# A four-block network on one Trainium2 core: the third block finishes its pairs of heads one pipeline step on, merges start two turns later, and ScalarE copies projections and u out of PSUM

## The chip, the cores and the metric

The kernel runs as one program on one core of a Trainium2 chip. The metric is the time of the program on the device in microseconds (us). The core's engines are named as in its profile: PE is TensorE, DVE VectorE, ACT ScalarE, POOL GpSimd, SP SyncE, which here only issues DMA transfers.

## The reference

A network of four residual blocks on x of 4 x 512 x 512, each `x = x + layernorm(block(layernorm(x)))`: a state-space block, a block with top-2 experts, a delta-rule attention and a block whose experts are chosen per sequence. The change is in the third alone. Of that block (16 heads of 128 channels, 512 tokens, everything in float32):

```python
q = silu(conv4(x @ Wq)); k = silu(conv4(x @ Wk)) * D ** -0.5; v = silu(conv4(x @ Wv))
alpha = sigmoid(x @ Wa + ba); beta = sigmoid(x @ Wb + bb)
def step(St, inp):                      # over the tokens
    sk = einsum('bhij,bhj->bhi', St, k_)
    err = sk - v_
    Sn = a_ * St - b_ * err[..., None] * k_[..., None, :]
    o_ = einsum('bhij,bhj->bhi', Sn, q_)
    return Sn, o_
o = layernorm_per_head(o) * ln_w + ln_b
g = sigmoid(x @ Wg)
return (o * g) @ Wo
```

`conv4` is a causal convolution over 4 tokens, one channel at a time.

## The kernel before

The four blocks run one after the other; the third, `delta_rule`, takes about 1143 to 3400 us of the profiled execution. It works on one sequence at a time (4 of them, 512 tokens, `xT` channel-major) and on two heads at a time: 32 steps of one pair each, and one more to drain. The token recurrence is cut into 4 chunks of 128 tokens (`TPB`), each solved as a triangular system. In step n:

- First part, run in turns. `in_turns` takes one piece (up to a `yield`) of each generator after another. `prepare` for both heads of pair n: three projections (`project`, L151) with their convolution and silu (`conv_silu`: ACT L156, DVE three times L158, ACT L162, POOL L163), the products k k and k q within a chunk (L672), weighted with decays to `lt` and `pt` (L675), the diagonal blocks of `lt` written to DRAM (L679), scaled copies `kq` (L685) and `kt` (L692, L694). With them `merge` for pair n-1: it puts the 32 x 32 inverses in `yi` together to 128 x 128 ones in five pieces (L752 to L804), with PE and ACT or DVE in turn.
- Second part, in turns: `solve` for pair n, which inverts the 32 x 32 blocks row by row on DVE (62 instructions, L720 and L727) and sends them through DRAM into `yi` (L732, L736); and `recur` for pair n-1, four chunks of r (ACT copy L830), u (DVE copy L840), new state S (DVE L847, L850) and output o (ACT copy L858), each after small products (L817).
- Then `finish` for pair n-1: `stats` (DVE L114, L115, POOL L117, L118) and `normalise` (DVE L122) over the eight 128 x 128 tiles of `o`; for both heads the gate projection with `wg` (L151), its sigmoid (L892), the transposes of `o` (L895), scale and shift (ACT L897), the product with the gate (POOL L898); then the products with `wo` (L903), added into `y` (L907 for the first pair, L909 for the others). After the last pair of a sequence, `residual` adds the normalised `y` to x.

The order that the code is written in is not the order of the engines. Instructions are placed ahead of time by a list planner: the place in the program is the priority, and an instruction that the planner takes for ready earlier, on durations that it assumes, can pass those before it. So the gate projections (L151 with `wg`) stand between the small products of the recurrence in the trace. On the chip each engine then keeps that order, and waits on semaphores.

What can pass is limited by buffers. PSUM has three for projections, L672 and the products with `wo` (`mm`), three for transposes and merges (`tr`), two for the recurrence (`sq`). In SBUF `cv`, `sg`, `wh`, `wg` and `wo` have two each, `o` and `gt` one. All loads of this block are issued by SP, in one queue: `wh` (L941), `wg` (L874), `wo` (L876), the decays `ag` (L639), and the way through DRAM (L679, L710, L732, L736).

Of the kernel before, what the change touches and what calls it, by code (L numbers as in the profile page):

```python
# [16 lines left out]
P = 128  # L17
# [59 lines left out]
def network(ctx: ExitStack, tc: tile.TileContext, a: dict, out: bass.AP):  # L77
# [75 lines left out]
    def conv_silu(pool, dst, p, w, bias):  # L153

        cv = pool.tile([P, S], F32, tag="cv", name="cv", bufs=2)
        nc.scalar.activation(cv, p, AF.Identity, bias=bias, scale=w[:, 3:4])  # L156
        for j in range(1, 4):
            nc.vector.scalar_tensor_tensor(  # L158
                cv[:, j:], p[:, : S - j], w[:, 3 - j : 4 - j], cv[:, j:], ALU.mult, ALU.add
            )  # L160
        sg = pool.tile([P, S], F32, tag="sg", name="sg", bufs=2)
        nc.scalar.activation(sg, cv, AF.Sigmoid)  # L162
        nc.gpsimd.tensor_tensor(dst, cv, sg, ALU.mult)  # L163
# [417 lines left out]
    def delta_rule():  # L581
        with (
# [22 lines left out]
            def decays(xT):  # L605
# [3 lines left out]
                al = bp.tile([H2, TPB, CP], F32, tag="al", name="al")  # L609
                nc.gpsimd.memset(al[:, :, 0:1], 0.0)  # L610
                nc.scalar.activation(al[:, :, 1:], chunk(zp), AF.Sigmoid, bias=ba)
                ga = bp.tile([H2, TPB * CP], F32, tag="ga", name="ga")
# [24 lines left out]
            def prepare(h, w, xT, dd, nb, blocks, out):  # L637
# [5 lines left out]
                for j, dst in ((1, qk[:, 0, :]), (0, qk[:, 1, :]), (2, vT)):  # L643
                    p = ps("mm")
                    project(p, lambda k: w[:, k, j, :], xT)
                    conv_silu(sp, dst, p, cw[:, j, h, :], cb[:, j, h : h + 1])
                    yield
# [90 lines left out]
            def merge(lts, yi):  # L738
# [10 lines left out]
                lo, hi = slice(0, 2 * BK), slice(2 * BK, P)  # L749
                xx = sp.tile([P, UNITS, 2 * BK], F32, tag="xx", name="xx", bufs=1)  # L750
# [56 lines left out]
            def recur(heads, yi, o):  # L807

                st = None
                for cc in range(TPB):  # L810
# [29 lines left out]
                    nc.vector.tensor_copy(  # L840
# [40 lines left out]
            def finish(o, ws, wos, pair, xT, y):  # L881
# [5 lines left out]
                gated = []  # L887
                for j in range(2):
                    p = ps("mm")
                    project(p, lambda k: ws[j][:, k, :], xT)  # L890
                    gt = sp.tile([P, S], F32, tag="gt", name="gt", bufs=1)
                    nc.scalar.activation(gt, p, AF.Sigmoid)  # L892
                    p = ps("tr")
                    for cc in range(TPB):
                        nc.tensor.transpose(one(p, cc), o[:, cc, j, :], ident)  # L895
                    oT = sp.tile([P, S], F32, tag="oT", name="oT", bufs=2)
                    nc.scalar.activation(oT, p, AF.Identity, bias=lnb, scale=lnw)  # L897
                    nc.gpsimd.tensor_tensor(oT, oT, gt, ALU.mult)  # L898
                    gated.append(oT)
                for i in range(TPB):  # L900
# [7 lines left out]
                    else:  # L908
                        nc.vector.tensor_tensor(y[i], y[i], p, ALU.add)  # L909

# [14 lines left out]
            before = None  # L925
            for n in range(B * NPAIR + 1):
                b, pair = divmod(n, NPAIR)
                now, parts, heads = None, [], []
                if n < B * NPAIR:
                    if pair == 0:  # L930
# [3 lines left out]
                        y = [  # L934
                            bp.tile([P, D], F32, tag=f"y3{i}", name=f"y3{i}") for i in range(TPB)
                        ]
# [9 lines left out]
                    now = (heads, inverses[n % 2], b, pair, xT, y)  # L946
                if before:
                    gates = gate_weights(before[3])
                    parts.append(merge([head[0] for head in before[0]], before[1]))
                in_turns(*parts)  # L950
                parts = []
                if now:
                    parts.append(solve(blocks, now[1]))
                if before:
                    o = sp.tile([P, TPB, 2, P], F32, tag="o", name="o", bufs=1)
                    parts.append(recur([head[1] for head in before[0]], before[1], o))
                in_turns(*parts)
                if before:
                    finish(o, *gates, *before[3:])
                    if before[3] == NPAIR - 1:  # L960
                        for i in range(TPB):
                            residual(bp, before[2] * TPB + i, before[5][i])
# [230 lines left out]
```

## Time and profile before

| | |
|---|---|
| median of 3 runs | 3653.46 us (3652.5 to 3656.45) |
| profiled execution, its own time | 3652.81 us |
| its span in the trace | 3651.0 us |
| mean granted TensorE clock | 0.907 |
| busy PE / DVE / ACT / POOL | 3179.4 / 2064.8 / 799.0 / 953.5 us |
| third block | about 1143 to 3400 us |
| L151 with `wh` | 1536 products of 128 x 512, 607 ns each |
| L158 | 672, 744 ns each (576 of them in this block) |
| L903 | 512 products of 128 x 512, 738 ns each |
| L895 | 256 transposes, 467 ns each |

A float32 product appears as two records, so a projection of four products is eight. A row of the waits names the engine and line that waited, then who ended the wait, total us, times and longest. A row of the timeline gives start, duration, engine, line, operation, output and inputs, shape, how many were merged, and in square brackets the idle time before the first and who ended it. A product's own duration reaches past the start of the next one; how fast a row of them runs is read from start to start.

### The profile page before, as it was taken

To read this page: it belongs to the slowest core of one execution; us is meant where nothing else is said; L and a number is where in the kernel's file an instruction comes from. 1 tells how busy PE (TensorE), PEld (TensorE's weight loads), DVE (VectorE), ACT (ScalarE), POOL (GpSimd) and SP (SyncE) were. 2 spreads that over 40 slices of the span, in tenths; PEclk is the share of its full clock that TensorE was granted. 3 is DMA by queue.
4 is the path that set the end of the run, shared out by engine and by line. 5 is a ranking of instruction groups with operands and counts; after the bars stand their busy time and mean duration, and the time that the engine had idled before them with its cause. 6 is when DMAs were issued, how large, how long until landed. Compare 5 with 4: busy or idle time off the path is not lost.

```text
span 3651.0 us, 39495 instructions
## 1 busy us (share of the span) xinstructions
PE 3179.4 (87%) x13779; PEld 1752.8 (48%) x13779; DVE 2064.8 (57%) x5189; ACT 799.0 (22%) x1399; POOL 953.5 (26%) x1018
## 2 busy tenths in 40 slices
PE   7889989899995889989989989889899989897268
PEld 3333344455552455555555645555555545555123
DVE  4556441311125667676766666766676767664852
ACT  2223211111110222222222222222222222221111
POOL 1322120300016323322423222323223323221112
PEclk9889989999997889989989989989999989998679
DMA  6000010389973322322322322323322323220300
GB/s 239 0 1 0 0 50 0 137 285 319 319 262 93 81 63 60 90 60 54 82 63 64 89 59 53 83 60 80 73 60 64 78 60 77 69 60 22 107 12 35
DMA packets 281240, 316.23 MB, mean 87 GB/s; under 512 B 119073, under 2 KB 184993, under 8 KB 281042
## 3 DMA queue, kind: packets, MB, share of 16 engines
q1 hardware_dynamic: 266496, 277.62, 26.7%
q10 hardware_dynamic: 9426, 19.31, 1.4%
q0 software_dynamic: 5120, 16.78, 1.4%
q8 instruction: 110, 1.80, 0.2%
q14 instruction: 88, 0.72, 0.1%
HBM read 271.95 MB, written 41.68 MB: 86 GB/s over the span
## 4 chain that ended last, share of the span: by engine, by line
PE 75%; DVE 12%; POOL 6%; issue 3%; ACT 3%; DMA 2%; SPq 0%; POOLq 0%; ACTq 0%; DVEq 0%
PE mm L151 32%; PE sq L817 7%; PE mm L903 7%; PE mm L512 5%; PE mm L672 3%; PE sq L534 3%; PE sq L276 2%; POOL rs L118 2%; PE tr L358 2%; PE sq L1086 2%; DVE o L122 2%; DVE prod L997 2%; DVE term L720 1%; DVE st L114 1%; DVE xb L727 1%
## 5 line engine op out<-in xcount | busy, mean ns | idle before, releaser
L151 PE MATMUL mm<-xT,wh 128*128 128x512 f32 x1536 | 691.2, 607 | 2.2 <-DVE cv L158 2.0
L158 DVE SCALAR_TENSOR_TENSOR cv<-mm,prm,cv 128x511 f32<-128x511 f32 (+2 forms) x672 | 499.3, 744 | 289.2 <-ACT cv L156 275.1
L151 PEld LDWEIGHTS mm<-xT,wh 128*128 128x128 f32 x1536 | 294.4, 194 | 364.8 <-issue 357.6
L903 PE MATMUL mm<-wo,oT 128*128 128x512 f32 x512 | 293.9, 738 | 60.0 <-POOL oT L898 60.0
L156 ACT ACTIVATE cv<-mm,prm 128x512 f32<-128x512 f32 x224 | 172.6, 771 | 524.1 <-PE mm L151 516.7
L720 DVE TENSOR_TENSOR term<-lb,xb 128x60 f32<-128x60 f32 (+24 forms) x992 | 257.7, 260 | 20.5
L151 PE MATMUL mm<-xT,wg 128*128 128x512 f32 x512 | 262.2, 600 | 0.7 <-ACT gt L892 0.7
L727 DVE TENSOR_TENSOR xb<-xb,term 128x60 f32<-128x60 f32 (+24 forms) x992 | 223.7, 226 | 24.7
L903 PEld LDWEIGHTS mm<-wo,oT 128*128 128x128 f32 x512 | 120.0, 242 | 216.8 <-issue 139.2
L163 POOL TENSOR_TENSOR qk<-cv,sg 128x512 f32<-128x512 f32 x128 | 162.5, 1269 | 201.5 <-ACT sg L162 201.4
L895 PE MATMUL tr<-const,o 128*128 128x128 f32 x256 | 101.8, 467 | 111.9 <-DVE o L122 111.1
L162 ACT ACTIVATE sg<-cv 128x512 f32<-128x512 f32 x224 | 140.4, 627 | 256.6 <-DVE cv L158 255.6
L512 PE MATMUL mm<-gu,rT 128*128 128x352 f32 x624 | 190.9, 459 | 0.2 <-ACT rT L508 0.2
L151 PE MATMUL mm<-xT,gu 128*128 128x512 f32 (+1 forms) x384 | 176.2, 618 | 12.6 <-DVE act L353 12.6
L512 PEld LDWEIGHTS mm<-gu,rT 128*128 128x128 f32 x624 | 118.2, 190 | 76.5 <-issue 17.8
L817 PE MATMUL sq<-S,kq 128*128 128x128 f32 x768 | 154.5, 283 | 0.0
L117 POOL TENSOR_SCALAR rs<-mv 128x1 f32<-128x1 f32 (+2 forms) x112 | 30.9, 276 | 449.1 <-DVE mv L115 448.9
L672 PE MATMUL mm<-qk 128*128 128x128 f32 x1024 | 137.8, 283 | 6.3 <-POOL vT L163 2.9
L276 PE MATMUL sq<-w_out,G 128*128 128x512 f32 x256 | 128.0, 651 | 13.4 <-POOL G L272 11.7
L546 POOL DMA_INDIRECT got<-yg,index x32 | 38.1, 1189 | 362.5 <-DMA yg<-yo 345.4
L163 POOL TENSOR_TENSOR vT<-cv,sg 128x512 f32<-128x512 f32 x64 | 100.2, 1565 | 115.3 <-ACT sg L162 115.3
L672 PEld LDWEIGHTS mm<-qk 128*128 128x128 f32 x1024 | 123.9, 194 | 11.0 <-POOL vT L163 3.1
(231 smaller groups left out, 4891.2 us busy)
## 6 DMA issues: line engine op xcount, KB each, us to landing
gu<-in_gu SPq DMA_DIRECT2D x86, 704.0 KB
wh<-in_wh SPq DMA_DIRECT2D x64, 768.0 KB
ag<-dd SPq DMA_DIRECT2D x64, 516.0 KB
dn<-in_dn SPq DMA_DIRECT2D x43, 512.0 KB
wg<-in_wg SPq DMA_DIRECT2D x64, 256.0 KB
wo<-in_wo SPq DMA_DIRECT2D x64, 256.0 KB
lb<-blocks SPq DMA_DIRECT2D x128, 128.0 KB
xg<-zero SPq DMA_DIRECT2D x3, 3328.0 KB
```

Of the source, the lines that this page charges most:

```text
L151: nc.tensor.matmul(dst, lhsT=w(k), rhs=xT[:, k, :], start=k == 0, stop=k == n - 1)
L156: nc.scalar.activation(cv, p, AF.Identity, bias=bias, scale=w[:, 3:4])
L158: nc.vector.scalar_tensor_tensor(cv[:, j:], p[:, : S - j], w[:, 3 - j : 4 - j], cv[:, j:], ALU.mult, ALU.add)
L162: nc.scalar.activation(sg, cv, AF.Sigmoid)
L163: nc.gpsimd.tensor_tensor(dst, cv, sg, ALU.mult)
L276: nc.tensor.matmul(po, lhsT=G[ct][:, i * P : (i + 1) * P], rhs=w_out[:, ct, :], start=ct == 0, stop=ct == NCT - 1,)
L512: nc.tensor.matmul(dst, lhsT=rT[:, k, :], rhs=gu[:, k, lo : lo + F], start=k == 0, stop=k == KD - 1)
L672: nc.tensor.matmul(one(p, cc), lhsT=one(kT, cc), rhs=one(rhs, cc), start=True, stop=True)
L720: nc.vector.tensor_tensor(term, lb[:, i : i + 1, i + 1 :].to_broadcast([P, n, left]), xb[:, :n, i : i + 1].to_broadcast([P, n, left]), ALU ...
L727: nc.vector.tensor_tensor(rest, rest, term, ALU.add)
L817: nc.tensor.matmul(p[:, j, :], lhsT=lhsT, rhs=rhs, start=n == 0, stop=n == len(terms) - 1,)
L903: nc.tensor.matmul(p, lhsT=one(gated[j], i), rhs=wos[j], start=j == 0, stop=j == 1)
```

## The change

`finish` loses its first part, the statistics and normalisation of `o`, to a new function `centred`, which stays after the recurrence. What is left of `finish` becomes a generator and runs one step later, as the first of the parts that take turns with `prepare` and `merge`: pair n-2's gates and output products beside the projections of pair n. The loop gets one more step to drain. The loads of `wg` and `wo` move with it. `y` is allocated where it is first needed, and the residual of a sequence follows each product of the last pair. `o` and `gt` get two buffers; `al` and `ga` share the two of `xn`. `merge` waits two turns before its first piece. In this block `conv_silu` lets ScalarE copy the projection from PSUM into `sg`, and the convolution reads `sg`. The copy of u moves from VectorE to ScalarE.

```diff
--- before.py
+++ after.py
@@ -150,15 +150,19 @@
         for k in range(n):
             nc.tensor.matmul(dst, lhsT=w(k), rhs=xT[:, k, :], start=k == 0, stop=k == n - 1)
 
-    def conv_silu(pool, dst, p, w, bias):
+    def conv_silu(pool, dst, p, w, bias, apart=False):
+
 
         cv = pool.tile([P, S], F32, tag="cv", name="cv", bufs=2)
+        sg = pool.tile([P, S], F32, tag="sg", name="sg", bufs=2)
+        if apart:
+            nc.scalar.copy(sg, p)
+            p = sg
         nc.scalar.activation(cv, p, AF.Identity, bias=bias, scale=w[:, 3:4])
         for j in range(1, 4):
             nc.vector.scalar_tensor_tensor(
                 cv[:, j:], p[:, : S - j], w[:, 3 - j : 4 - j], cv[:, j:], ALU.mult, ALU.add
             )
-        sg = pool.tile([P, S], F32, tag="sg", name="sg", bufs=2)
         nc.scalar.activation(sg, cv, AF.Sigmoid)
         nc.gpsimd.tensor_tensor(dst, cv, sg, ALU.mult)
 
@@ -606,10 +610,10 @@
 
                 zp = ps("sq")[:H2, :]
                 project(zp, lambda k: wab[:, k, 0:H2], xT)
-                al = bp.tile([H2, TPB, CP], F32, tag="al", name="al")
+                al = bp.tile([H2, TPB, CP], F32, tag="xn", name="al", bufs=2)
                 nc.gpsimd.memset(al[:, :, 0:1], 0.0)
                 nc.scalar.activation(al[:, :, 1:], chunk(zp), AF.Sigmoid, bias=ba)
-                ga = bp.tile([H2, TPB * CP], F32, tag="ga", name="ga")
+                ga = bp.tile([H2, TPB * CP], F32, tag="xn", name="ga", bufs=2)
                 flat = al.rearrange("h c t -> h (c t)")
                 nc.vector.tensor_tensor_scan(ga, flat, c("pad1")[:H2], 0.0, ALU.mult, ALU.add)
                 dd = dram.tile([2, H2, TPB * CP], F32, tag="dd", name="dd")
@@ -643,7 +647,7 @@
                 for j, dst in ((1, qk[:, 0, :]), (0, qk[:, 1, :]), (2, vT)):
                     p = ps("mm")
                     project(p, lambda k: w[:, k, j, :], xT)
-                    conv_silu(sp, dst, p, cw[:, j, h, :], cb[:, j, h : h + 1])
+                    conv_silu(sp, dst, p, cw[:, j, h, :], cb[:, j, h : h + 1], apart=True)
                     yield
                 kT, qT = qk[:, 0, :], qk[:, 1, :]
 
@@ -747,6 +751,8 @@
 
                 q = [slice(n * BK, (n + 1) * BK) for n in range(NB)]
                 lo, hi = slice(0, 2 * BK), slice(2 * BK, P)
+                for _ in range(2):
+                    yield
                 xx = sp.tile([P, UNITS, 2 * BK], F32, tag="xx", name="xx", bufs=1)
                 nc.gpsimd.memset(xx[q[0], :, BK:], 0.0)
                 nc.vector.transpose(xx[q[0], :, :BK], yi[q[0], :, q[0]])
@@ -837,7 +843,7 @@
                         ),
                     )
                     u = sp.tile([P, 2, P], F32, tag="u", name="u")
-                    nc.vector.tensor_copy(
+                    nc.scalar.copy(
                         u, pair(lambda j, vT, pt, kq, gc, kt: [(yi[:, j * TPB + cc, :], r[:, j, :])])
                     )
                     if cc < TPB - 1:
@@ -878,25 +884,33 @@
                     wos.append(wo)
                 return ws, wos
 
-            def finish(o, ws, wos, pair, xT, y):
+            def centred(o):
 
                 rows = [(cc, j) for cc in range(TPB) for j in range(2)]
                 mv, rs = stats([o[:, cc, j, :] for cc, j in rows], EPS / P, "o")
                 for n, (cc, j) in enumerate(rows):
                     normalise(o[:, cc, j, :], o[:, cc, j, :], mv, rs, n)
-                gated = []
+
+            def finish(o, ws, wos, b, pair, xT, y):
+
+                gates = []
                 for j in range(2):
                     p = ps("mm")
                     project(p, lambda k: ws[j][:, k, :], xT)
-                    gt = sp.tile([P, S], F32, tag="gt", name="gt", bufs=1)
+                    gt = sp.tile([P, S], F32, tag="gt", name="gt", bufs=2)
                     nc.scalar.activation(gt, p, AF.Sigmoid)
+                    gates.append(gt)
+                    yield
+                gated = []
+                for j in range(2):
                     p = ps("tr")
                     for cc in range(TPB):
                         nc.tensor.transpose(one(p, cc), o[:, cc, j, :], ident)
                     oT = sp.tile([P, S], F32, tag="oT", name="oT", bufs=2)
                     nc.scalar.activation(oT, p, AF.Identity, bias=lnb, scale=lnw)
-                    nc.gpsimd.tensor_tensor(oT, oT, gt, ALU.mult)
+                    nc.gpsimd.tensor_tensor(oT, oT, gates[j], ALU.mult)
                     gated.append(oT)
+                yield
                 for i in range(TPB):
                     p = ps("mm")
                     for j in range(2):
@@ -907,6 +921,10 @@
                         nc.scalar.copy(y[i], p)
                     else:
                         nc.vector.tensor_tensor(y[i], y[i], p, ALU.add)
+                    if pair == NPAIR - 1:
+                        residual(bp, b * TPB + i, y[i])
+                    if i % 2:
+                        yield
 
             def in_turns(*parts):
                 parts = list(parts)
@@ -922,8 +940,9 @@
 
 
 
-            before = None
-            for n in range(B * NPAIR + 1):
+
+            before = last = None
+            for n in range(B * NPAIR + 2):
                 b, pair = divmod(n, NPAIR)
                 now, parts, heads = None, [], []
                 if n < B * NPAIR:
@@ -931,9 +950,6 @@
                         xT = bp.tile([P, KD, S], F32, tag="xT3", name="xT3", bufs=2)
                         norm_transposed(bp, xT, b)
                         dd, nb = decays(xT)
-                        y = [
-                            bp.tile([P, D], F32, tag=f"y3{i}", name=f"y3{i}") for i in range(TPB)
-                        ]
                     blocks = dram.tile([2, TPB, NB, BK, BK], F32, tag="blocks", name="blocks")
                     for j in range(2):
                         h = 2 * pair + j
@@ -943,23 +959,27 @@
                             a["wh"][h].rearrange("(k p) c -> p k c", p=P),
                         )
                         parts.append(prepare(h, w, xT, dd, nb, blocks[j], heads))
-                    now = (heads, inverses[n % 2], b, pair, xT, y)
+                    now = (heads, inverses[n % 2], b, pair, xT)
                 if before:
-                    gates = gate_weights(before[3])
                     parts.append(merge([head[0] for head in before[0]], before[1]))
+                if last:
+                    if last[2] == 0:
+                        y = [
+                            bp.tile([P, D], F32, tag=f"y3{i}", name=f"y3{i}") for i in range(TPB)
+                        ]
+                    o, at, of, x_of = last
+                    parts.insert(0, finish(o, *gate_weights(of), at, of, x_of, y))
                 in_turns(*parts)
-                parts = []
+                parts, last = [], None
                 if now:
                     parts.append(solve(blocks, now[1]))
                 if before:
-                    o = sp.tile([P, TPB, 2, P], F32, tag="o", name="o", bufs=1)
+                    o = sp.tile([P, TPB, 2, P], F32, tag="o", name="o")
                     parts.append(recur([head[1] for head in before[0]], before[1], o))
                 in_turns(*parts)
                 if before:
-                    finish(o, *gates, *before[3:])
-                    if before[3] == NPAIR - 1:
-                        for i in range(TPB):
-                            residual(bp, before[2] * TPB + i, before[5][i])
+                    centred(o)
+                    last = (o, *before[2:])
                 before = now
 
 
```

## Prediction

> **What bounds the kernel now.** I read the busy table first, then the waits of stage 3 (1143 to 3400 us), then one step of its loop in the timeline, then that step's granted clock. A 65 us step, one pair of heads, runs 32 times.
>
> The busy table, engine by engine:
>
> ```profile
> PE 3179.4 (87%) x13779; PEld 1752.8 (48%) x13779; DVE 2064.8 (57%) x5189; ACT 799.0 (22%) x1399; POOL 953.5 (26%) x1018
> ```
>
> TensorE is the busiest. The waits in stage 3 (total us, times, longest) name two places where TensorE itself stops:
>
> ```profile
> PE tr L895 <- DVE o L122: 111.1, 32, 3.9
> PE mm L903 <- POOL oT L898: 60.0, 32, 2.0
> ```
>
> That is 3.5 and 1.9 us, once per pair, both in `finish`. The larger waits in that list belong to ScalarE, GpSimd or the load queue, which have time to spare. The TensorE timeline of one step:
>
> ```profile
> 1837.60 0.61 PE L817 MATMUL sq<-const,vT 128*128 128x128 f32 x4
> 1841.65 3.24 PE L895 MATMUL tr<-const,o 128*128 128x128 f32 x8 [3.44 <-DVE o L122]
> 1846.75 10.13 PE L903 MATMUL mm<-wo,oT 128*128 128x512 f32 x16 [1.87 <-POOL oT L898]
> 1856.72 13.90 PE L151 MATMUL mm<-xT,wh 128*128 128x512 f32 x32
> ```
>
> The recurrence ends, TensorE waits 3.44 us, transposes at VectorE's pace, waits 1.87 us, and multiplies by `wo`. Then 16 products take 10.13 us where 32 of the same shape take 13.90 next (0.434 each, so 6.95 for 16). The cause is in the clock (columns: stretch, its us, PE busy, PEclk, DMA share, GB/s):
>
> ```profile
> 1370.00:1376.00 6.00, 5.05 (x7) 0.59 0.00 0
> 1376.00:1380.10 4.10, 4.10 (x11) 1.00 0.01 2
> ```
>
> After the pauses the clock is 0.59, then 1.00 again. Whole steps (PE, PEld, DVE, ACT, POOL busy, clock):
>
> ```profile
> 1906.70:1971.90 65.20, 59.44 (x322) 35.47 (x322) 45.05 (x131) 15.87 (x29) 19.75 (x21) 0.92 0.30 71
> 1971.90:2037.00 65.10, 59.29 (x322) 35.34 (x322) 44.81 (x130) 15.86 (x29) 19.82 (x21) 0.92 0.30 72
> ```
>
> What TensorE needs at full clock: `wh` 48 x 0.434 = 20.9; `wg` and `wo` 16 each, 6.95 twice; recurrence 84 x 0.111 = 9.3; L672 3.8; merge 4.2; transposes 1.7. Sum 53.8 of 65.2: 11.4 us per pair are lost.
>
> [...]0.59 after the pauses, 0.50 in 1777.2 to 1779.5. [...]in the step shown L720, two SBUF inputs, took 1.22 us where its neighbours took 0.23, until GpSimd's L898 (1845.44, 1.26 us) ended, within 0.1 us; L158, with its second input in PSUM, took 0.75 at 1864.90 beside GpSimd's L163. [...]The trace has 0.68 (L302, SBUF) against 0.745 (L158).
>
> **The change part by part.**
>
> 1. `finish` moves a step on. The transposes of `o` now follow both gate projections and four `wh` projections: 6 x 8 x 0.434 = 20.8 us of TensorE work that doesn't need `o`. Some is drawn into the recurrence, as all 16 `wg` products (6.9 us) are today, but at least 10 us must be left. From the recurrence's end (1838.2) to the last normalised `o` (1844.4) are 6.2 us: covered. Removed per pair: the wait 3.5; transposes at 3.24 instead of 8 x 0.11, 2.3; the wait for L898, 1.9, covered by the v projections (7 us) that follow in the same turn; the slow clock, from five steps (9.04, 9.10, 9.09, 10.13, 9.48; mean 9.37 - 6.95, less 0.1 by which the rows overlap), 2.3. **Sum 10.0.** If the v projections come earlier, the L898 wait stays.
> 2. `wg` and `wo` loads: still four per pair on SP, now in the step that uses them, behind the `wh` loads. SP stood 634.6 us in 58 waits for a `wo` buffer, longest 29.5; `ag`, `blocks<-lt`, `solved` and `yi` queue behind. At best this gains (in this step `solved` left at 1856.44, 1.7 after its data), at worst gates or blocks come late: -1 to +4 per pair, I take 0.
> 3. GpSimd: the same two L898 (2 x 1.28), now ahead of products for q, k, v; cover is 65 - 20 us of idle GpSimd. The same pow of L118; its 1.66 us is no longer waited for.
> 4. Merges two turns on: no instruction more. Their last two rounds lose the projections beside them: 2 x (ScalarE 0.58 + about 0.3 hand-over) = 1.8 us if nothing fills in; the first recurrence and gate products can. 0 to 3, I take 0.7. The reason to wait is in the profile: `yi` comes some 42 us after `lt` (1821.2 to 1863.4).
> 5. ScalarE copies: 192 x 0.586 (as L131, L907) and 128 x 0.372 for u: 3.5 + 1.5 per pair, plus 0.2 for an SBUF source; busy 16 to 21, of 56. Hidden by its idle time; a projection lags 0.6 us more, covered by three PSUM buffers. In exchange a PSUM buffer is free after one copy instead of after L156 and three L158. The u copies leave VectorE: -1.7; on the chain 0.37 for 0.42.
> 6. L158 from SBUF: 18 x 0.065 = -1.2 of VectorE; but L158 now contends with GpSimd. GpSimd's large instructions per pair: 6 x 1.27 + 4 x 0.95 + 2 x 1.05 + 2 x 1.28 = 16.1. Blocked time is from 0 to 16; VectorE spends some 28 of 56 us on two SBUF inputs (L158 12, solve 13, scans 2.5), half of the time, so 8, of which about 3 are paid today (L720's two of a microsecond, L658, L163). +5: VectorE 44.9 - 2.9 + 5 = 47 of 56. Not the bound, but late now and then: 0 to 5 on TensorE, I take 1.3.
> 7. `al` and `ga` share two `xn` buffers: four times, 0 to 3 us each. Second buffers for `o` and `gt`: nothing. The extra loop turn: its `finish` stood after the last recurrence before too. The last pair's gap stays: 31 gains.
>
> Net per pair 10.0 - 0.7 - 1.3 = 8.0, a step of about 57 us. 31 x 8.0 = 248. The profiled execution took 3652.81 (span 3651.0 and 1.8 around it); the median shown is 3653.46, within 0.65. 3652.8 - 248 = **3405 us**.
>
> **The rivals.** (A) The forecast, some 3320 to 3460. For it: outside the finish TensorE lost only about 1.4 us per step, so the order was good where it had work to draw on.
>
> (B) The gap is partly replaced. Either the merge's tail stands bare (3 us) with `yi` late[...]. Net 4 to 5.5 per pair: 3482 to 3529. For: the order is made ahead, from planned costs, and 20 us of VectorE idle stand in today's step. Against: ScalarE now empties PSUM, so TensorE can run up to five projections ahead of VectorE.
>
> (C) Slower[...]. Place: L158 with two SBUF inputs beside L163 and L685. Price: all 16.1 us blocked less the 3 paid, 44.9 - 2.9 + 13 = 55, and half of today's 20.3 us of idle remaining, 65.2; it decides when new waits and idle together pass 65.2 - 42 = 23.2 us per pair. With 13 of each it is 68: 31 x 2.8 = 87, 3740. For: L720 shows a wait to five times its length. Against: it needs nearly every GpSimd instruction to hit.
>
> (D) It doesn't do what it says: the planned order places gates and projections inside the recurrence and leaves the wait for `o`, moved but as long. Then only parts 5 and 6 act, within 10 us of 3653. Against: PSUM buffers bound what can be drawn ahead.
>
> **How the numbers follow.** A 0.68, B 0.22, C 0.06, D 0.04. D is split between 0.2% (7 us, about what a measurement of this kernel can tell from no change) and gains or losses beyond, C is slower: faster 0.91, same 0.03, slower 0.06. The low end is all of 10.0 and 0.8 of the 1.4 lost elsewhere, nothing paid: 31 x 10.8 = 335, 3318, rounded to 3320; the high end takes in B: net 4, 3530. Outside are C, D and the tails of A and B.
>
> **What would show it.** Right: the two finish waits gone (L895 on `o`, L903 on L898, together below 30 us), L895 near 280 ns a product, L903 near 600 instead of 738, clock above 0.96 in stage 3, a step of 56 to 58 us, ScalarE busy near 959. Part 6 shows as a longer L158 or L163. The forecast is wrong if TensorE waits over 4 us per step on L158, L163, `yi` or a `wg` load, or L158 averages over 1.1 us.

## The result, and the profile after

The changed kernel took **3705.0 us** (median of 4 runs, 3704.2 to 3714.9), the kernel before 3653.0 in the same comparison (4 runs, 3651.9 to 3656.5): ratio 1.0147, 95% interval 1.0129 to 1.0165. The forecast was 3405. The change made the kernel slower, by 52 us or 1.5%.

The busy table of the changed kernel, and then the shares of the chain that ended last, by engine:

```profile
PE 3171.8 (86%) x13779; PEld 1769.5 (48%) x13779; DVE 2129.5 (58%) x5061; ACT 952.2 (26%) x1719; POOL 988.1 (27%) x1018
```

```profile
DVE 29%; PE 26%; ACT 3%; POOL 3%; issue 3%; DMA 1%; SPq 0%; DVEq 0%; ACTq 0%; POOLq 0%
```

The busy shares hardly moved. The chain did: before, 75% of it were TensorE and 12% VectorE. Now VectorE has the larger part (these shares add up to 65%; the page gives no engine for the rest).

The waits of TensorE in the third block (1143 to 3460 us; total us, times, longest):

```profile
PE mm L917 <- POOL oT L911: 74.5, 38, 4.7
PE mm L676 <- DVE y L923: 50.1, 32, 2.3
PE tr L130 <- DVE xn L122: 49.9, 4, 16.0
PE tr L908 <- DVE o L122: 22.3, 19, 8.8
PE mm L917 <- ACT sg L159: 20.1, 9, 2.6
```

Line numbers have moved: L908, L911 and L917 were L895, L898 and L903; L676 was L672, L923 was L909, and L724, L731 were L720, L727. The convolution's multiply-adds are now L163 (L158 before), the silu's last product L167 (L163 before). L159 is the new copy. The wait for `o` fell from 111.1 to 22.3, as planned. The wait for GpSimd's product did not go, it grew from 60.0. The waits for `y` and for the copy `sg` are new, and the one for `xn`, at the starts of the sequences, was 17.6.

Groups of the changed page (busy us, mean ns, idle before):

```profile
L163 DVE SCALAR_TENSOR_TENSOR cv<-sg,prm,cv 128x511 f32<-128x511 f32 (+2 forms) x576 | 511.7, 890 | 154.7 <-ACT cv L161 121.9
...
L917 PE MATMUL mm<-wo,oT 128*128 128x512 f32 x512 | 299.8, 719 | 96.1 <-POOL oT L911 74.5
...
L724 DVE TENSOR_TENSOR term<-lb,xb 128x60 f32<-128x60 f32 (+24 forms) x992 | 270.7, 273 | 19.5
L731 DVE TENSOR_TENSOR xb<-xb,term 128x60 f32<-128x60 f32 (+24 forms) x992 | 260.1, 262 | 20.4
```

L163 averages 890 ns where L158 took 744. The solve's two rows, L724 and L731, together take 530.8 us; they took 481.4. L917 still runs at 719 ns (738 before).

About thirty steps of the loop, before and then after, in one stretch of each trace (stretch, its us; busy PE, PEld, DVE, ACT, POOL; clock; DMA share; GB/s):

```profile
1300.00:3280.00 1980.00, 1793.60 (x9584) 1063.63 (x9585) 1354.79 (x3907) 485.72 (x883) 604.17 (x630) 0.91 0.28 69
```

```profile
1300.00:3280.00 1980.00, 1729.61 (x9334) 1055.84 (x9333) 1372.83 (x3677) 603.37 (x1139) 619.84 (x619) 0.92 0.27 67
```

TensorE is idle 186 us of the 1980 before and 250 after. From the first transpose of `o` to that of the last pair are 31 steps: 66.8 us each before, 68.1 after. Per step TensorE's idle time went from 6.3 to 8.6 us and VectorE's work from 45.7 to 47.2.

**One step after the change.** TensorE, ScalarE, GpSimd and VectorE in the same 15 us (start us, us, engine, line, operation, count, idle before and its releaser):

```profile
1932.56 1.04 PE L908 MATMUL tr<-const,o 128*128 128x128 f32 x8
1933.44 7.03 PE L151 MATMUL mm<-xT,wh 128*128 128x512 f32 x16
...
1946.02 5.41 PE L917 MATMUL mm<-wo,oT 128*128 128x512 f32 x6 [4.69 <-POOL oT L911]
```

```profile
1940.83 0.63 ACT L166 ACTIVATE sg<-cv 128x512 f32<-128x512 f32 x1 [3.96 <-DVE term L724]
...
1942.07 0.76 ACT L910 ACTIVATE oT<-tr,prm 128x512 f32<-128x512 f32 x1
```

```profile
1941.53 1.27 POOL L167 TENSOR_TENSOR qk<-cv,sg 128x512 f32<-128x512 f32 x1 [3.31 <-ACT sg L166]
1942.88 1.42 POOL L689 TENSOR_TENSOR kq<-qk,ag 128x384 f32<-128x384 f32 x1
1944.26 1.70 POOL L911 TENSOR_TENSOR oT<-oT,gt 128x512 f32<-128x512 f32 x1
```

```profile
1939.98 0.75 DVE L163 SCALAR_TENSOR_TENSOR cv<-sg,prm,cv 128x509 f32<-128x509 f32 x1
...
1941.50 0.17 DVE L724 TENSOR_TENSOR term<-lb,xb 128x8 f32<-128x8 f32 x1
1941.71 1.13 DVE L731 TENSOR_TENSOR xb<-xb,term 128x8 f32<-128x8 f32 x1
1942.75 3.76 DVE L163 SCALAR_TENSOR_TENSOR cv<-sg,prm,cv 128x511 f32<-128x511 f32 x3
```

All transposes of `o` are done at 1933.6. The second scaled copy of them, L910, starts at 1942.07: on ScalarE it stands behind the silu's sigmoid L166, which waits for a convolution (L163) that VectorE only gets to between rows of the solve. (The bracket of L166 names the row L724 that ran just then; what L166 reads is `cv`, and the last L163 on it ended at 1940.73.) Then GpSimd's product L911 stands behind L167 and L689 of that same convolution. TensorE, which had covered 7 us with projections, runs out of other work and waits 4.69 us; its next six products take 0.90 us each instead of 0.43, at a granted clock of 0.50 (1946.1 to 1951.2). ScalarE itself sat idle for 3.96 us before L166, though L910 had its input all that time. So the wait for GpSimd is here at its root a wait for VectorE. This is the longest of the 38 waits; in 35 of them GpSimd went into L911 straight from L689 or from the other L911, and the transposes of `o` had been done for 7 us or more. The same excerpt shows VectorE's instructions grow beside GpSimd's: a solve row of 8 columns (L731 at 1941.71) takes 1.13 us, until L167 ends at 1942.80, where the row before it took 0.17; and three L163 take 3.76 beside L689 and L911, where three L158 took 2.31 in the kernel before.

### The profile page after: what moved, and what is told of

The parts are those of the page before. It is cut to its first block, busy times and chain, and to the rows that moved or that the text cites. A ratio compares the mean times of both kernels' runs of the same rounds, so it can differ in the third digit from the quotient of the medians.

```text
span 3701.7 us, 39645 instructions
## 1 busy us (share of the span) xinstructions
PE 3171.8 (86%) x13779; PEld 1769.5 (48%) x13779; DVE 2129.5 (58%) x5061; ACT 952.2 (26%) x1719; POOL 988.1 (27%) x1018
## 4 chain that ended last, share of the span: by engine, by line
DVE 29%; PE 26%; ACT 3%; POOL 3%; issue 3%; DMA 1%; SPq 0%; DVEq 0%; ACTq 0%; POOLq 0%
DVE cv L163 10%; PE mm L151 7%; DVE term L724 5%; DVE xb L731 5%; PE mm L917 4%; PE sq L823 4%; DVE o L122 2%; PE mm L676 2%; POOL rs L118 2%; PE sq L1106 2%; DVE prod L1017 2%; ACT cv L161 2%; DVE st L114 1%; DMA yi<-solved 1%; PE tr L766 1%
## 5 line engine op out<-in xcount | busy, mean ns | idle before, releaser
L151 PE MATMUL mm<-xT,wh 128*128 128x512 f32 x1536 | 716.9, 600 | 1.6 <-ACT gt L901 0.8
L163 DVE SCALAR_TENSOR_TENSOR cv<-sg,prm,cv 128x511 f32<-128x511 f32 (+2 forms) x576 | 511.7, 890 | 154.7 <-ACT cv L161 121.9
L151 PEld LDWEIGHTS mm<-xT,wh 128*128 128x128 f32 x1536 | 275.5, 193 | 254.3 <-issue 249.2
L917 PE MATMUL mm<-wo,oT 128*128 128x512 f32 x512 | 299.8, 719 | 96.1 <-POOL oT L911 74.5
L167 POOL TENSOR_TENSOR qk<-cv,sg 128x512 f32<-128x512 f32 x128 | 164.1, 1282 | 587.5 <-ACT sg L166 579.3
L166 ACT ACTIVATE sg<-cv 128x512 f32<-128x512 f32 x224 | 140.9, 629 | 571.5 <-DVE cv L163 511.6
L724 DVE TENSOR_TENSOR term<-lb,xb 128x60 f32<-128x60 f32 (+24 forms) x992 | 270.7, 273 | 19.5
L731 DVE TENSOR_TENSOR xb<-xb,term 128x60 f32<-128x60 f32 (+24 forms) x992 | 260.1, 262 | 20.4
L151 PE MATMUL mm<-xT,wg 128*128 128x512 f32 x512 | 254.1, 611 | 1.7 <-DVE pt L679 0.9
L676 PE MATMUL mm<-qk 128*128 128x128 f32 x1024 | 170.9, 329 | 74.4 <-DVE y L923 50.1
L917 PEld LDWEIGHTS mm<-wo,oT 128*128 128x128 f32 x512 | 106.3, 227 | 237.6 <-POOL oT L911 116.0
L676 PEld LDWEIGHTS mm<-qk 128*128 128x128 f32 x1024 | 162.3, 241 | 104.6 <-DVE y L923 57.5
L151 PE MATMUL mm<-xT,gu 128*128 128x512 f32 (+1 forms) x384 | 175.2, 615 | 13.5 <-DVE act L357 13.5
L117 POOL TENSOR_SCALAR rs<-mv 128x1 f32<-128x1 f32 (+2 forms) x112 | 43.1, 385 | 424.8 <-DVE mv L115 424.5
L161 ACT ACTIVATE cv<-sg,prm 128x512 f32<-128x512 f32 x192 | 155.5, 810 | 3.6
L159 ACT COPY sg<-mm 128x512 f32<-128x512 f32 x192 | 112.0, 583 | 157.3 <-PE mm L151 127.7
L689 POOL TENSOR_TENSOR kq<-qk,ag 128x384 f32<-128x384 f32 x128 | 138.2, 1081 | 52.2 <-PE sq L823 45.0
L655 POOL TENSOR_TENSOR d<-const,nb 128x516 f32<-128x516 f32 x64 | 69.4, 1084 | 270.2 <-DVE m L662 230.7
L122 DVE TENSOR_SCALAR o<-o,mv,rs 128x128 f32<-128x128 f32 x256 | 109.9, 431 | 54.9 <-POOL rs L118 54.9
```

The costliest lines, as they stand in the source:

```text
L122: nc.vector.tensor_scalar(dst, src, mv[:, j, 0:1], rs[:, j : j + 1], ALU.subtract, ALU.mult)
L151: nc.tensor.matmul(dst, lhsT=w(k), rhs=xT[:, k, :], start=k == 0, stop=k == n - 1)
L163: nc.vector.scalar_tensor_tensor(cv[:, j:], p[:, : S - j], w[:, 3 - j : 4 - j], cv[:, j:], ALU.mult, ALU.add)
L676: nc.tensor.matmul(one(p, cc), lhsT=one(kT, cc), rhs=one(rhs, cc), start=True, stop=True)
L724: nc.vector.tensor_tensor(term, lb[:, i : i + 1, i + 1 :].to_broadcast([P, n, left]), xb[:, :n, i : i + 1].to_broadcast([P, n, left]), ALU ...
L731: nc.vector.tensor_tensor(rest, rest, term, ALU.add)
```

## Experiments: the copies, and VectorE beside GpSimd

**The change without the ScalarE copies of the projections**, everything else kept:

```
-  conv_silu(sp, dst, p, cw[:, j, h, :], cb[:, j, h : h + 1], apart=True)
+  conv_silu(sp, dst, p, cw[:, j, h, :], cb[:, j, h : h + 1])
```

> The changed kernel with the convolution reading PSUM again (no copy by ScalarE); finish, late merges and u on ScalarE stay. Theory 1 (VectorE is now the bound, on the way lt, DRAM, solve, convolutions, next lt[...]): L163 back at about 745 ns, the solve's instructions near 240 ns, and most of 156 us comes back, 3540 to 3600 us. Rival (the copy is what lets TensorE run ahead of VectorE; without it PSUM's three buffers are held through the convolutions and TensorE stalls): 3700 or more.

Measured: 3607.0 us, 0.9865 of before (0.9848 to 0.9881). The copies cost 98 us, 3.2 per step; without them the change is a gain of 46. The 156 us of the expectation are what L163, L724, L731 and L122 take longer than before by their means. The run ended just above theory 1's range, far below the rival's.

**The copies kept, but VectorE reads PSUM.** ScalarE still copies, and its own L161 reads the copy; the multiply-adds read the projection:

```
-  p = sg
-  nc.scalar.activation(cv, p, AF.Identity, bias=bias, scale=w[:, 3:4])
+  nc.scalar.activation(cv, sg if apart else p, AF.Identity, bias=bias, scale=w[:, 3:4])
```

> The changed kernel, in which ScalarE still copies each projection and L161 reads the copy, but the three instructions of the convolution on VectorE read PSUM: same copies, no second SBUF input on VectorE. [...]L163 back at 745 ns and 3600 to 3630 us, near the 3607 of the run without copies. Rival (the copies cost by their length on ScalarE and by the longer way from projection to silu): 3690 to 3720.

The first range is for the case that what the copies cost is the second SBUF input of L163. Measured: 3622.7 us, 0.9909 (0.9892 to 0.9925). Of the 98 us, 82 go when VectorE's multiply-adds read PSUM, though ScalarE copies as before; 16 stay with the copies. The planner laid VectorE's order anew in this run, so the 82 hold the SBUF source together with the order that comes with it. The same instruction in this kernel and in the changed one (duration ns min/median/max; in this kernel it stands on L162):

```profile
L162 DVE SCALAR_TENSOR_TENSOR cv<-mm,prm,cv x672: 692/747/751, 35.4 to 3250.7; 128x511 f32<-128x511 f32 x56, 128x510 f32<-128x510 f32 x56, 128x509 f32<-128x509 f32 x56
```

```profile
L163 DVE SCALAR_TENSOR_TENSOR cv<-sg,prm,cv x576: 694/749/1851, 1196.6 to 3337.8; 128x511 f32<-128x511 f32 x192
```

From PSUM no execution was longer than 751 ns; from SBUF the median is within 2 ns of it and the longest is 1851. The SBUF source made nothing shorter. Of its 576 executions in the changed kernel 167 took over 760 ns; each of these overlapped an instruction of GpSimd and ended 0.54 to 0.55 us after that one's end.

**The copies alone, in the kernel before:**

```
...
+  sg = pool.tile([P, S], F32, tag="sg", name="sg", bufs=2)
+  if apart:
+      nc.scalar.copy(sg, p)
+      p = sg
...
+  conv_silu(sp, dst, p, cw[:, j, h, :], cb[:, j, h : h + 1], apart=True)
```

> The kernel before with ScalarE's copies of the projections alone. Theory 1: VectorE has some 13 us of waits for L156 in a step[...]: +20 to +90 us, L158's line near 890 ns. Rival (the copies cost nothing and free PSUM early): 3653 or some 10 to 30 us less.

Measured: 3843.6 us, 1.0519 (1.0502 to 1.0537): 190 us, nearly twice their cost in the changed kernel and more than twice the 90 expected at most. VectorE, then GpSimd beside it:

```profile
1934.82 3.23 DVE L163 SCALAR_TENSOR_TENSOR cv<-sg,prm,cv 128x511 f32<-128x511 f32 x3 [1.02 <-ACT cv L161]
```

```profile
1934.09 1.27 POOL L167 TENSOR_TENSOR qk<-cv,sg 128x512 f32<-128x512 f32 x1 [1.29 <-ACT sg L166]
1935.44 1.28 POOL L689 TENSOR_TENSOR kq<-qk,ag 128x384 f32<-128x384 f32 x1
```

Three multiply-adds take 3.23 us where three took 2.31 in the kernel before, with GpSimd's two products of the projection before alongside. In the order of before, the projections of a pair stand close together, so the products of one fall on the convolution of the next. L163's mean is 998 ns here against 890 in the changed kernel. A second cost is in the trace: the copy L159 needs a free `sg`, and ScalarE stood 93.2 us in 94 waits for L167 to give one back (23.9 in 27 in the changed kernel). How the 190 divide between the two was not separated.

## Experiments: the finish, the merges, u

**The finish moved, and nothing else** (the changed kernel with three parts put back: merges not delayed, convolution from PSUM, u on VectorE).

> The kernel before with finish moved one step on alone: no late merges, convolution from PSUM, u on VectorE. If the late merges are what makes the move possible (without them the changed kernel took 3932, waiting 426 us for the transposes of yi)[...]: 3780 to 3860. If that wait came only from the longer solve[...]: 3600 to 3680.

Measured: 3947.7 us, 1.0796 (1.0766 to 1.0826), slower than either range.

**The whole change without the two idle turns of the merges:**

```
-  for _ in range(2):
-      yield
```

> The changed kernel without the two idle turns of merge. Theory 1: the merge is not what binds, within 20 us of 3705. Rival 2 (the late merge leaves TensorE's last merge rounds bare, so recurrence, the copy S of L853 and the solve queued behind it on VectorE start late; VectorE waited 178 us for L853 in 29 steps): about 3 us per step, 3600 to 3630. Rival 3 (the turns are there because yi comes late): slower than 3705 by 1 to 3 us per step, 3740 to 3800.

Measured: 3931.8 us, 1.0762 (1.0744 to 1.078). The two turns are worth 227 us, more than any of the three theories gave; rival 3 had the direction and the reason. Waits of TensorE in the third block, and one of them in its timeline (the merge's lines are two lower here, L764 and L756):

```profile
PE tr L764 <- DVE xx L756: 420.0, 28, 25.3
```

```profile
1948.77 1.06 PE L764 MATMUL tr<-xx,lt 32*32 32x32 f32 x16 [15.02 <-DVE xx L756]
```

L756 in turn starts when `yi` has arrived. Of the 15 us the first 5.6 pass until VectorE ends the last row of the solve (1939.31), the other 9 on the way through DRAM and into L756. `finish` had been doing a second job: while it ran, VectorE worked through the solve. With it moved away, the merge stands at the head of the next step and TensorE waits 15 us on average for `yi` (13 in the kernel with the finish alone: 376.6 us in 29 waits). Both pay it, so it comes from the moved finish, and the delayed merges are what repairs it. The copies and the move of u cost nothing in this order (3931.8 with them, 3947.7 without): the 98 us are their price in one order of work, not a fixed one. Part 4 of the forecast had seen the reason (`yi` some 42 us after `lt`) but booked the turns as a cost only.

**u copied by VectorE instead of ScalarE:**

```
-  nc.scalar.copy(
+  nc.vector.tensor_copy(
```

> The changed kernel with the copies of u back on VectorE. Theory 1: four copies of 0.42 us per step return to the engine that binds, less where VectorE waits in the recurrence anyway: 3705 to 3750. Rival (ScalarE's copies of u are queued behind L159 and L161 and hold up the recurrence): 3650 to 3690.

Measured: 3726.9 us, 1.0198 (1.0181 to 1.0215). Moving u to ScalarE gains 22 us, against the 1.7 us per step of VectorE's time that it frees (31 x 1.7 = 53).

## Experiments: what bounds the rest

Without the copies 3607 us were left where the forecast stood at 3405. The next runs ask which engine's work sets the step now.

**TensorE's work cut.** The gate projections sum 1 product instead of 4 (the gates are left incomplete):

```
-  project(p, lambda k: ws[j][:, k, :], xT)
+  project(p, lambda k: ws[j][:, k, :], xT, 1)
```

> The changed kernel with each gate projection cut to the first of its four products (the sum over the other channels left out): 12 records of 0.434 = 5.2 us per step less on TensorE, nothing less on VectorE. VectorE theory (solve and convolutions in a row on VectorE set the step, TensorE waits for their results through ScalarE's and GpSimd's queues): 0 to 1 us per step, 3670 to 3710. Rival (TensorE is still the bound): most of 5.2 us, 3540 to 3590.

Measured: 3674.3 us, 1.0051 (1.0035 to 1.0068): 31 us gained for 185 us of TensorE work removed (the row of L151 with `wg` fell from 254.1 to 69.3). The time came back as waits for VectorE:

```profile
PE tr L908 <- DVE o L122: 141.4, 46, 8.0
PE mm L676 <- DVE y L923: 67.8, 46, 3.5
```

**VectorE's work cut, at the end of the recurrence.** The normalisation of `o` is left out:

```
-  centred(o)
```

> The changed kernel without the statistics and the normalisation of o (left out), which are 8 x 0.43 + 16 small instructions, some 7 us of VectorE per step, and the wait of 1.7 us for GpSimd's pow. Loop theory (VectorE's work between solve and lt binds): 5 to 8 us per step less, 3450 to 3550. Rival (TensorE's order or the merges bind, VectorE only looks busy): within 40 us of 3705.

Measured: 3571.3 us, 0.9769 (0.9746 to 0.9791): 134 gained for 220 us of VectorE rows removed (L122 109.9, L114 68.1, L115 41.6). With them went GpSimd's L117 and L118 for `o`, for which VectorE had waited 54.9 us, so the 134 are not the price of VectorE's rows alone.

**VectorE's work cut in the solve.** The first 16 of its 31 rows are left out, in the changed kernel and in the one without copies:

```
-  for i in range(BK - 1):
+  for i in range(BK // 2, BK - 1):
```

> The changed kernel with the first 16 of the 31 elimination rows of solve left out: 32 instructions and some 8 us per step less on VectorE, nothing less on TensorE. VectorE theory: at least half of it comes back, as it did without the normalisation (134 us of some 7 us per step), 4 to 8 us per step, 3450 to 3580. Rival (TensorE, or the order of the queues whatever VectorE has to do): 3670 to 3710.

> The version whose convolution reads PSUM (3607 us), with the first 16 of the 31 rows of solve left out, some 8 us of VectorE per step. If what is left between 3607 and the forecast of 3405 is VectorE being late (by ring or by work in a row): 3440 to 3510. If it is TensorE and the order of the queues: 3580 to 3620.

Measured: 3555.3 us, 0.9729 (0.9696 to 0.9762), and 3424.9, 0.9362 (0.9344 to 0.938). The two rows fell by 279 us (530.8 to 251.5) and by 347 (588.6 to 241.4); the gains are 150 and 182, the second a little more than expected.

Side by side, in us:

| run | engine | its work removed | time gained | share |
|---|---|---|---|---|
| gates cut | TensorE | 185 | 31 | 17% |
| no normalisation of o | VectorE | 220 | 134 | 61% |
| half the solve | VectorE | 279 | 150 | 54% |
| half the solve, no copies | VectorE | 347 | 182 | 52% |

In these cuts a microsecond of VectorE is worth three of TensorE, though VectorE is busy 69% of the stretch shown above and TensorE 87%. Two reservations: the planner may lay the order anew when instructions go, and that part was not separated; and leaving out solve rows also brings `yi` sooner. The next runs were meant for the second; neither settles it.

**yi from an earlier solve**, so that the merges need not wait for this pair's way through DRAM (the results of the pair before are used), with and without copies:

```
-  view = solved.rearrange("(u n) m g t -> n (m g) u t", n=NB)
+  view = (kept[-1] if kept else solved).rearrange(
+      "(u n) m g t -> n (m g) u t", n=NB
+  )
+  kept.append(solved)
...
```

> The changed kernel, in which yi is filled from the solved blocks of the pair before (the wrong inverses), so that merge doesn't wait for this step's solve and its way through DRAM. Ring theory (a step is solve 29 us, DRAM to yi 9, transposes and merge 20, the first piece of the recurrence, and on VectorE behind it the next solve: 62 us in the step from 1913.66 to 1975.9): the ring is open, 3 us per step or more, 3450 to 3620. Rival (what VectorE has to do in a row from solve to lt binds, whenever yi comes): within 40 us of 3705.

> The same on the version whose convolution reads PSUM (3607 us): yi from the pair before. Ring theory: 3 us per step or more, 3420 to 3520. Rival: 3570 to 3640.

Measured: 3687.8 us, 1.0068 (1.0046 to 1.009), and 3575.0, 0.9779 (0.9763 to 0.9796): gains of 17 and 32. **Inconclusive** on the ring solve, DRAM, `yi`, merge, next products: `yi` did not come earlier. SP's queue in the first of the two:

```profile
1948.25 2.52 SPq L736 DMA_DIRECT2D solved<-xb  x4
...
1952.14 1.83 SPq L743 DMA_DIRECT2D yi<-solved  x4
```

The last row of the solve ended at 1948.23, and the loads of `yi`, though they read older blocks, still stand in SP's queue behind this step's writes of `solved`; in every step of both runs they left 3.9 us or more after those, as in the changed kernel. The planner also moved the merges: L761 starts at 1972.95, long after `yi` came. So the ring was neither opened nor excluded.

**The solve reads the blocks of the step before**, to take the first half of that way out:

```
-  parts.append(solve(blocks, now[1]))
+  parts.append(solve(older or blocks, now[1]))
+  older = blocks
...
```

> The changed kernel, in which solve reads the blocks that the step before wrote to DRAM, so its inverses belong to the wrong pair, and the way lt, DRAM, lb no longer stands between one step's lt and the same step's solve. Loop theory (a step is the DRAM way, some 13 us in which VectorE has little to do, and then solve and convolutions in a row on VectorE until the next lt): 4 to 9 us per step less, 3430 to 3580. Rival (VectorE's dense part or TensorE binds whatever the DRAM way): within 40 us of 3705.

Measured: 3726.5 us, 1.0197 (1.018 to 1.0214). **Inconclusive**: SP's queue shows that the load did not come earlier.

```profile
1966.02 1.74 SPq L683 DMA_DIRECT2D blocks<-lt  x4
...
1972.60 1.71 SPq L714 DMA_DIRECT2D lb<-blocks  x4
```

The loads of `lb` still stand behind this step's writes of `blocks`, so the wait was not taken away.

## Experiments: a faster version

**The normalisation of o on ScalarE**, without the projection copies (two small GpSimd operations make the bias):

```
-  normalise(o[:, cc, j, :], o[:, cc, j, :], mv, rs, n)
+  nc.scalar.activation(
+      o[:, cc, j, :], o[:, cc, j, :], AF.Identity,
+      bias=ms[:, n : n + 1], scale=rs[:, n : n + 1],
+  )
...
```

> The changed kernel with the convolution reading PSUM (as in the run of 3607 us), and the eight normalisations of o on ScalarE (scale rs, bias -mean times rs, two small GpSimd instructions for it) instead of VectorE. Loop theory: 8 x 0.34 = 2.7 us per step leave VectorE, 3607 - 84 = 3523, from 3510 to 3560. Rival[...]: 3590 to 3625, or slower if the longer GpSimd chain is felt by the transposes.

Measured: **3581.9 us**, 0.9799 (0.9782 to 0.9815): faster than both kernels, 71 us below before and 25 below the version without copies, which is between the two ranges expected. In the stretch 1300 to 3280 us TensorE is idle 179 us and its clock is 0.96.

**A third `cv` buffer on top of it** (`conv_silu(..., nb=3)`):

> The changed kernel with the convolution from PSUM and the normalisation of o on ScalarE (3582 us), and a third buffer for cv, so that one more projection can be drawn ahead and PSUM is freed without waiting for the silu two projections back. If TensorE's waits for mm buffers behind L163 (some 2 us per step) are from cv's two buffers: 3530 to 3565. If they are from VectorE being late in any case: 3570 to 3590.

Measured: 3589.2 us, 0.9804 (0.9778 to 0.983), no different from the run without it. In this version the buffer was not what held the convolutions.

## Why the prediction was wrong

Two terms of the sum failed, parts 1 and 6, on one judgment, which stands in **part 6**: VectorE at 47 of 56 is "Not the bound, but late now and then: 0 to 5 on TensorE, I take 1.3". The 47 was met (47.2 measured), but the step was not 56. It was reasoned from a busy share. VectorE idles some 21 us per step before and after. Before, its longest waits in the stretch shown were those of the convolutions for ScalarE (198.9 of 625 us); after, those of the state S for TensorE's small products (L853 and L856, 230 of 607) and of the convolutions (100). That time is waiting for other engines, and the runs that cut work say that it was not room for other work.

The measured time lies 300 us above the forecast. 98 of them go with the copies: the SBUF source that part 6 priced at 1.3 us per step cost 2.6 in the changed kernel (82 / 31), with the copies 3.2 (98 / 31); source and copies together cost 6.1 in the kernel before (190 / 31).

The other 202 stay without the copies, and their place is part 1. With all idle time before the `wo` products counted, the finish brought 100 us in the changed kernel and 107 without the copies, 3.2 and 3.5 per pair of the 10.0 forecast. In the changed kernel its cover fails in the queues, at L911. Without the copies the wait for L911 is only 4.3 us, but TensorE stops before the same products for a PSUM buffer, 102 us in 51 waits. TensorE, and VectorE just before, in that version:

```profile
1984.35 2.90 PE L917 MATMUL mm<-wo,oT 128*128 128x512 f32 x3 [3.30 <-issue]
```

```profile
1983.50 0.75 DVE L163 SCALAR_TENSOR_TENSOR cv<-mm,prm,cv 128x509 f32<-128x509 f32 x1
```

26 of the waits (28.7 us) the trace puts down to L163. For the other 25 (73.5 us) it names nothing, but each ended 0.1 us after the end of an L163, the instruction that reads the projection last and so frees its buffer. Either way it is a late convolution on VectorE.

By its own parts:

1. **The finish.** Forecast 10.0 per pair. The wait for `o` fell by 88.8 us in all; the transposes by 53.6 (101.8 to 48.2, now 304 ns each against some 280 expected). The wait for GpSimd's product rose by 14.5 and the `wo` products took 5.9 longer, so the 1.9 and the 2.3 did not come at all. Sum 122 us, 3.9 per pair. Here the word "covered" (by the v projections) failed. TensorE's 7 us were there, but ScalarE's L910 and GpSimd's L911 stood in order behind work that waits for VectorE.
2. **Loads of `wg` and `wo`**, taken at 0: TensorE's list of waits names neither. Held, as far as that list shows.
3. **GpSimd's L911 "ahead of products for q, k, v"**: in the step shown, and in nearly all others, it comes behind two of them. Wrong.
4. **Merges.** Taken at a cost of 0.7; the run without the turns lost 227 us. They are the part without which the change is 7.6% slower.
5. **ScalarE** busy 952, forecast 959. Right as a sum; hidden, except for some 16 us. The early release of PSUM did come: TensorE waited 29 us for the copy L159, where without it L163 held it 102 us before the `wo` products alone. It was bought with VectorE's longer instructions of part 6. The 0.2 per pair for an SBUF source came as well: L161, which reads the copy, averages 810 ns, L156 on PSUM 771, so six cost 0.23.
6. **The SBUF source.** The gain of 65 ns per multiply-add, for which the trace of before had only L302 (0.68, another shape) against L158 (0.745), did not come: medians 749 ns from SBUF and 747 from PSUM. That the multiply-adds would grow beside GpSimd did: from PSUM none took over 753 ns (752 before, 751 with the copies and a PSUM source, 753 in the other blocks of the changed kernel), from SBUF up to 1851 in the changed kernel. But part 6 counted only instructions with two SBUF inputs, which was the author's estimate, from L720 and L158 of the trace before; L122 on `o`, a TENSOR_SCALAR with one tensor input, also took up to 1289 ns beside GpSimd (last section). The added waits were forecast at 5 us per step on VectorE. L163 (428.0 to 511.7 from the run without copies), the solve (481.4 to 530.8 from before) and L122 on `o` (86.3 to 109.9) rose by 157 together, 4.9 per pair. That this meets the 5 is partly luck: only 84 of it, 2.6 per pair, are on the instruction that part 6 meant, and the solve is longer still without the copies. What the waits cost in time was mis-sized in any case.

What TensorE gained at the finish (122) it lost elsewhere: idle time before L676 rose by 68 us (6.3 to 74.4), other idle time before L917 by 22 (96.1 less 60.0 and the 14.5 above), and L676 and L151 with `wh` took 33 and 26 longer, in all 149. That is 27 more than was gained, of the 51 us between the two profiled spans. The largest of the other rows is at the starts of the last three sequences, L130 on `xn`. TensorE stands 11.3 us each time until VectorE has normalised the next x. Before, this wait was 0.5 us: `finish` of the sequence's last pair filled the time (L903 from 1695.72 to 1704.41, then these transposes). That makes 32 us, the version without the copies has them too, and the forecast has no term for them. The two together pass the 51; rows that got shorter were not all added up.

**The rivals.** C is the one that happened, in direction and by its engine: VectorE's lateness made the kernel slower, through L163 beside L167 and L689, and its 3740 was 35 off. That closeness is largely luck, for its working did not happen: it needed 13 us of waits beside GpSimd and half of VectorE's idle time gone. About five came, and the idle time stayed whole. B had the merge's tail and VectorE replacing part of the gap; without the copies the kernel shows what B describes, yet at 3607, above B's end of 3529.

Of the signs named in advance, the transposes (304 ns), ScalarE's busy time and the longer multiply-adds came out; the two finish waits did not (96.8 us together, against 30), nor L917 near 600 ns, a clock above 0.96 and a step of 57. The signs of failure were badly chosen: TensorE waits little on L163 by name, and L163 averages 0.89, below the 1.1 set as a limit. The damage reached TensorE through L910, L911 and L923.

**Still open**: which of VectorE's queue places costs most, and what the ring through DRAM costs. About half of VectorE's work removed came back as time, a sixth of TensorE's; no run kept the work and changed only the order in which solve rows and convolutions alternate.

## What to carry to other kernels

In this kernel VectorE, idle for 31% of the stretch, held up the busiest engine: L910 and L911 stood in ScalarE's and GpSimd's order behind instructions that waited for its results, and TensorE waited 74.5 us for L911. So follow the wait for GpSimd or ScalarE back through the queue before calling it covered, and test by removing work from each engine in turn. Before copying a PSUM operand to SBUF to free PSUM, count what reads it: here the copy became a second SBUF input of VectorE's multiply-adds, and their mean went from 744 to 890 ns, all executions over 760 beside GpSimd. A stage that is moved away may have been the cover for other work and its transfer (the two turns that repaired it were worth 227 us here); look for what finishes and what arrives while it runs. When a load is pointed at older data, check in its queue that it does leave earlier: those of `yi` still left 3.9 us or more behind the writes.

## What the runs showed of the hardware that was not expected

The solve, whose instructions did not change, got longer in the new order. The version without copies (busy us, mean ns):

```profile
L731 DVE TENSOR_TENSOR xb<-xb,term 128x60 f32<-128x60 f32 (+24 forms) x992 | 303.0, 305 | 18.6
L724 DVE TENSOR_TENSOR term<-lb,xb 128x60 f32<-128x60 f32 (+24 forms) x992 | 285.6, 288 | 18.4
```

That is 588.6 us against 481.4 before and 530.8 with the copies. In the step shown above a product of GpSimd falls beside the solve, and a row of 8 columns takes 1.13 us where the one before took 0.17. In all, 139 of the solve's 1984 executions took over 400 ns in the changed kernel and 78 before, and each ended within 0.1 us of the end of an instruction of GpSimd. With the second SBUF input taken away from the convolutions, L163 fell from 511.7 us to 428.0 and the solve rose from 530.8 to 588.6.

L122 on `o`, with one tensor input, went from 339 ns before and in the version without copies to 431 in the changed kernel and 428 with the copies but a PSUM source; so its length follows the order, not the source of L163. In the changed kernel 30 of its 256 executions took over 450 ns. VectorE, and GpSimd beside it:

```profile
1996.54 1.28 DVE L122 TENSOR_SCALAR o<-o,mv,rs 128x128 f32<-128x128 f32 x1 [1.74 <-POOL rs L118]
```

```profile
1996.47 1.27 POOL L167 TENSOR_TENSOR qk<-cv,sg 128x512 f32<-128x512 f32 x1
```

All 30 began within 0.1 us after the start of an L167 or L689 of GpSimd and ended within 0.1 us after its end; none of the other 226 lies inside an instruction of GpSimd. Before, none of the 256 met a large instruction of GpSimd, and none took over 347 ns. So in this kernel an instruction with a single tensor input in SBUF took longer beside GpSimd as well, up to 1289 ns, until GpSimd's instruction ended.
